# Reordering the last two pairs' products and changing how a list scheduler ranks what feeds small products, in a Winograd-like adaLN/FFN kernel

## The chip, the cores and the metric

The kernel runs on one NeuronCore of a Trainium2 chip. The metric is device time in microseconds of one execution; before the change the median of three runs is 460.26 us (460.14 to 460.26).

## The reference

All arrays are float32. `x` is 64 x 64 x 1024; each of the 64 batches has a condition number that picks one of sixteen 64 x 64 matrices.

```python
h = jnp.einsum('bct,bcd->bdt', x, cond_weights[condition])        # 64x64 matrix per batch
gate_logits = jnp.einsum('bsd,ed->bse', h, gate_w)                # 8 experts
weights, selected = jax.lax.top_k(gate_logits, 2)
w_full = sum(one_hot(selected) * softmax(weights))
low = jnp.einsum('bsd,erd->ebsr', h, lora_A)                      # 8 experts x rank 16
result = jnp.einsum('bsd,od->bso', h, base_w) + base_b
result += 2.0 * jnp.einsum('ebsr,eor,bse->bso', low, lora_B, w_full)
out = x + result
```

## The kernel before

**Tiling.** The 4096 tokens are 32 tiles of 128. The big product multiplies x (before the condition matrix, which is applied afterwards) with the 1160 columns of `lora_A`, `gate_w` and `base_w`, laid out as three column chunks of 384, 388 and 388. The contraction over 1024 is cut in four blocks of 256. float32 precision is kept by splitting each operand into a high and a low fp32r part: ScalarE (ACT) copies the high part (`xh`, `wh`, `zh`, line 234), VectorE (DVE) subtracts for the low part (`xl`, `wl`, `zl`, line 231), and TensorE (PE) does three matmuls for one product (line 414: high x high, low weight, low x).

**Plain tiles and pairs.** Tiles 0 to 3 are multiplied plainly, in the order of the list `PLAIN`: for tiles 0 and 1 the third column chunk takes the blocks in the order `LASTK = (3, 2, 0, 1)`, so its last weight block to arrive is `b23`. Tiles 4 to 31 go in 14 pairs (numbers 2 to 15) by a fast scheme with 20 products `p1` to `p20` for each pair. Each product is six matmuls of 388 (or 384) columns, in two halves. Four PSUM banks hold running sums, named X, Y, R and Q (`BANK`): several products of a pair add into one bank one after another. Between two of them an eviction takes the running sum out: DVE `mix` (line 740, writes `st`), ACT `keep` (line 719, writes `st`, recorded at line 234) or ACT `pass_on` (line 723, from bank to bank). The next product into the bank must wait for that eviction. In bank Y stand p19, p14, p15, p2, p8 and p9; an eviction follows each but p8. In bank X stand p16, p5, p17, p18, p3, p10 and p12.

**Small products.** When a chunk of z (the result of the big product) is complete, `chunk` splits it (`zh`, `zl`) and `post` applies the condition matrix (`bdh`, `bdl`) to it and adds the LoRA part: line 447, three to six matmuls into the banks `ps_a` and `ps_o`. Chunk 0 also feeds the gate (lines 486 to 493) and a transpose on PE (`tr`, line 500). `finish` (line 457) adds the result to the token tile `xtok`. The condition matrices are fetched by an indirect DMA from GpSimd (POOL, line 394, `bdr`) and split by `load_cond`: ACT `bdh`, DVE `bdl`. `load_tok` loads the x rows (SP, line 380) and adds the bias by DMA (POOL, line 381).

**What sets the order.** Nothing is ordered by the hardware: each engine executes its list of instructions in order, and waits at each for its operands. The lists are made when the program is built, by `Program.run`, a list scheduler with costs and due times written in the source. Each step gets a latest start `late` from the due times backwards through what depends on it. At every turn the engine that can start earliest takes, of its ready steps, one marked `first`, or else the one with the smallest `late`. The mark `first` is on the small products and transposes of tiles 0 to 29 (line 450 and `tr`); such a step is offered to PE only `MARGIN = 1.2` us after its operands are ready by the scheduler's own clock, and then goes ahead of the big products. Steps with `early` (loads and gathers) are offered not before `late - AHEAD`. The big products themselves are chained by the key `"order"`, so their order is exactly the hand-written list: `HEAD` and `TAIL` for pairs 2 to 13, and `FINAL` for the last two pairs, where `t` names a tail product of pair 14 and `p` a product of pair 15.

Of the kernel before, what the change touches and what calls it, by code (L numbers as in the profile page):

```python
# [41 lines left out]
PE, ACT, DVE, POOL, SP = "PE", "ACT", "DVE", "POOL", "SP"  # L42
# [4 lines left out]
ISSUE = 0.45  # L47
FLIGHT, DMA = 2.0, 1 / 360e3
QUEUE = 3.0
FIRST = 11.0  # L50
TWICE = 2.5
AHEAD = 10.0
MARGIN = 1.2
# [9 lines left out]
            p12="f9", p13="f13", p14="r", p15="f15", p16="a11", p17="a22", p18="f18", p19="f19", p20="f11")  # L63
BANK = dict(p6="R", p16="X", p7="Q", p5="X", p19="Y", p17="X", p11="R", p13="R", p18="X", p4="Q", p20="Q", p3="X",
            p1="R", p10="X", p12="X", p14="Y", p15="Y", p2="Y", p8="Y", p9="Y")
# [4 lines left out]

PARTS = ((2, slice(0, 200)), (2, slice(200, W)))

FINAL = "t14 p6 t15 p16 p7 t2 p5 t8 p17 t9 p11 p4 p13 p19 p18 p20 p14 p3 p10 p15 p12 p1 p2 p8 p9".split()

SPLITS = (("f6", "a11"), ("s", "f5"), ("f19", "a22"), ("f11", "f13"), ("f18", "a24"), ("f3", "f1"), ("a13", "f9"),
          ("r", "f15"), ("f2", "f8"))
# [3 lines left out]
class Program:  # L80
# [7 lines left out]
    def add(self, engine, cost, fn, reads=(), writes=(), due=None, first=False, size=0.0, early=None, port=False,  # L88
            after=0.0):

        n = len(self.steps)
        engine, cost = (e if isinstance(e, (list, tuple)) else [e] for e in (engine, cost))
        deps = set()
        for b in list(reads) + list(writes):
            if b in self.writer:
                deps.add(self.writer[b])
        for b in writes:
            deps.update(self.readers.get(b, ()))  # L100
        for b in reads:
            self.readers.setdefault(b, []).append(n)
        for b in writes:
            self.writer[b], self.readers[b] = n, []
        deps.discard(n)
        self.steps.append(dict(eng=dict(zip(engine, cost)), fn=fn, deps=deps, first=first, size=size, port=port,
                               lag=FLIGHT + QUEUE + size * DMA if size else 0.0, after=after,
                               due=self.horizon if due is None else due,
                               early=SP in engine and not reads if early is None else early))

    def run(self):
        steps, n = self.steps, len(self.steps)
        succ = [[] for _ in steps]
        for i, s in enumerate(steps):
            for d in s["deps"]:
                succ[d].append(i)
        hop = lambda a, b: SAME[a] if a == b else HOP[a]
        late = [0.0] * n
        for i in reversed(range(n)):
            s = steps[i]  # L120
            c, e = min(s["eng"].values()), next(iter(s["eng"]))
            late[i] = min([s["due"] - c] + [late[j] - hop(e, next(iter(steps[j]["eng"]))) - s["lag"] - c
                                            for j in succ[i]])
        left = [len(s["deps"]) for s in steps]
        ready, end, by = [0.0] * n, [0.0] * n, [None] * n
        free = dict(START)
        cand = {e: set() for e in HOP}

        def offer(i):
            for e in steps[i]["eng"]:  # L130
                t = max([steps[i]["after"]] + [end[d] + hop(by[d], e) for d in steps[i]["deps"]])
                if steps[i]["early"]:
                    t = max(t, late[i] - AHEAD)
                t += MARGIN if steps[i]["first"] else 0.0
                cand[e].add((i, t))

        for i in range(n):
            if not left[i]:
                offer(i)
        done, port, wire = 0, 0.0, 0.0  # L140
        while done < n:
            best = None
            for e, c in cand.items():
                if c:
                    t = max(free[e], min(max(r, port) if steps[i]["port"] else r for i, r in c))
                    if best is None or t < best[0]:
                        best = (t, e)
            t, e = best
            i, r = min(((i, r) for i, r in cand[e] if (max(r, port) if steps[i]["port"] else r) <= t + 1e-9),
                       key=lambda q: (not steps[q[0]]["first"], late[q[0]], q[0]))  # L150
            for f in steps[i]["eng"]:
                cand[f] = {q for q in cand[f] if q[0] != i}
            end[i], by[i] = t + steps[i]["eng"][e], e
            free[e] = end[i]
            if steps[i]["size"]:
                end[i] = wire = max(end[i] + FLIGHT, wire) + steps[i]["size"] * DMA
            if steps[i]["port"]:
                port = end[i]
            steps[i]["fn"](e)
            done += 1  # L160
            for j in succ[i]:
                left[j] -= 1
                if not left[j]:
                    offer(j)
        return max(end)
# [3 lines left out]
def cond_ffn_kernel(ctx, tc, xT, x, idx, cw, wall, bias, lb, out):  # L169
# [22 lines left out]
    eng = {ACT: nc.scalar, DVE: nc.vector, POOL: nc.gpsimd}  # L192
# [3 lines left out]
    def many(n, shape, dt, name):  # L196
        return [sb.tile(shape, dt, name=f"{name}{j}") for j in range(n)]
# [8 lines left out]
    bdr, bdh, bdl = many(2, [P, P], F32, "bdr"), many(2, [P, P], F32R, "bdh"), many(2, [P, P], F32R, "bdl")  # L206
# [21 lines left out]
    add = pr.add  # L228

    def sub(e, o, a, b):  # L230
        eng[e].tensor_tensor(o, a, b.bitcast(F32), ALU.subtract)  # L231

    def copy(e, o, a):
        (nc.scalar.copy if e == ACT else nc.vector.tensor_copy)(o, a)  # L234
# [7 lines left out]
    def tt_cost(n):  # L242
        return 0.08 + 0.00104 * n
# [94 lines left out]
    def mix_w(o, a, b, f, over):  # L338
# [3 lines left out]
        add(DVE, tt_cost(2 * W), lambda e: nc.vector.tensor_tensor(r.ap(), x.ap(), y.ap(), f),  # L342
            [k for z in (x, y) if z is not r for k in z.keys], r.keys, port=True, after=FIRST)

# [46 lines left out]
    def load_cond(i):  # L391

        j = i % 2
        add(POOL, 1.04, lambda e: nc.gpsimd.indirect_dma_start(  # L394
            out=bdr[j], out_offset=None, in_=cw,
            in_offset=bass.IndirectOffsetOnAxis(ap=rows[:, i:i + 1], axis=0)),
            ["rows"], [("bdr", j)], size=4.0 * P * P, early=True)
        add(ACT, 0.28, lambda e: copy(e, bdh[j], bdr[j]), [("bdr", j)], [("bdh", j)])
        add(DVE, 0.25, lambda e: sub(e, bdl[j], bdr[j], bdh[j]), [("bdr", j), ("bdh", j)], [("bdl", j)], port=True)


    due = {}
# [147 lines left out]
    for q in range(NPLAIN, NPAIR):  # L550
        if q == NPAIR - 2:
            ORDER += [(q + (p[0] == "p"), "p" + p[1:]) for p in FINAL]
            break
# [41 lines left out]
    add(POOL, 1.1, make_rows, writes=["rows"])  # L595
    add(POOL, 0.6, lambda e: make_identity(nc, ident), writes=["ident"])
    load_cond(0)
    load_cond(1)
    for k in LASTK:
        load_split_w(f"b{k + 1}3")  # L600
# [11 lines left out]
    def plain(i, c, k):  # L612
        if (i, k) not in xa0:
            us = xrs.two()
            for d in range(2):
                load_x(i, k + d, us[d])
            xa0[i, k], xa0[i, k + 1] = split_x(us)
            xrs.give(*us)
        if (i, c) not in zb:
            zb[i, c] = f"z{take('z', 4)}"  # L620
            if c == 0 and i > 1:
                load_cond(i)
        ks, m = LASTK if c == 2 and i < 2 else range(KQ), f"b{k + 1}{c + 1}"
        for f in range(2):
            zstep(("plain", i, c, k, f), zb[i, c], xa0[i, k], SINGLE.get(m, m), f, k == ks[0] and f == 0,
                  k == ks[-1] and f == 1, CN[c])
        left[i, k] -= 1
        if not left[i, k]:
            xas.give(xa0[i, k])
        if k == ks[-1]:  # L630
            post(i, c, split_z(CN[c], lambda: bank[zb[i, c]][:, :CN[c]], zb[i, c]))
            if c == 2:
                late_sum(i)
                store(i, range(3))
# [229 lines left out]
```

## Time and profile before

| | |
|---|---|
| median of three runs | 460.26 us |
| the profiled execution, as a run | 460.46 us |
| its span, first to last instruction | 458.7 us |
| outside of the span | 1.8 us |
| PE busy (matmuls) | 452.7 us, 99% |
| DVE busy | 383.5 us, 84% |
| ACT busy | 227.2 us, 50% |
| POOL busy | 89.6 us, 20% |
| granted TensorE clock | 1.000 |
| DMA traffic | 75.00 MB, mean 164 GB/s |

Times in the trace are microseconds from the start of the span. PE is the matmul row and PEld the row of weight loads, which runs ahead of it. A matmul is recorded with 0.34 us, but the next one starts 0.18 us later, since they overlap; so one reads the pace of PE from the starts. In brackets stands the idle time of an engine ahead of an instruction, with what ended it. Bank X is `ps_z` like all four; products are told apart by their weights: p10 is `wh_t_p` with 384 columns, p8 `wh_t_p` near the end, p9 `wh_g_p`, p15 `wh_h_p`.

### The profile page before, as it was taken

The numbers are of one execution on the slowest core, as the hardware profiler recorded it, in microseconds if no ns is written. First come the engines' busy times: TensorE is split into PE (matmuls) and PEld (weight loads), VectorE is DVE, ScalarE is ACT, GpSimd is POOL, SyncE is SP. The second block draws the span as 40 slices with busy tenths as digits, with TensorE's granted clock in tenths as the row PEclk, the third lists the DMA queues.
The fourth block names the chain that finished last, engine by engine and source line by source line (L and its number), as shares of the span: only waits on it lengthen the run. The fifth ranks groups of instructions, "written<-read, shape, count | busy, mean of one in ns | idle before, by whom it ended". The sixth has DMA issues, their size and how long they took to land.

```text
span 458.7 us, 7577 instructions
## 1 busy us (share of the span) xinstructions
PE 452.7 (99%) x2621; PEld 449.7 (98%) x2621; DVE 383.5 (84%) x941; ACT 227.2 (50%) x520; POOL 89.6 (20%) x107
## 2 busy tenths in 40 slices
PE   8999999999999999999999999999999999999995
PEld 8999999999999999999999999999999999999995
DVE  5999997879989788796987979789797988888674
ACT  5864666543736345373543646354454544546331
POOL 3030214121303021220303003030210403103000
PEclk9999999999999999999999999999999999999999
DMA  8932748977768462764847456565565746556142
GB/s 279 352 117 47 153 107 198 213 211 202 180 206 202 172 161 87 217 131 163 199 127 202 108 182 148 172 162 133 191 123 185 173 129 193 116 174 149 51 134 91
DMA packets 36229, 75.00 MB, mean 164 GB/s; under 512 B 4432, under 2 KB 22240, under 8 KB 36192
## 3 DMA queue, kind: packets, MB, share of 16 engines
q0 software_dynamic: 10560, 36.72, 33.5%
q1 hardware_dynamic: 25200, 37.32, 25.9%
q10 hardware_dynamic: 432, 0.49, 0.4%
q8 instruction: 20, 0.33, 0.3%
q14 instruction: 17, 0.14, 0.1%
HBM read 57.74 MB, written 16.78 MB: 162 GB/s over the span
## 4 chain that ended last, share of the span: by engine, by line
PE 97%; DMA 1%; DVE 1%; ACT 0%; issue 0%
PE ps_z L414 76%; PE ps_o L447 15%; PE ps_a L447 6%; DMA w_b<-in_w 1%; PE ps_a L500 1%; DVE wl_b_b L231 0%; DVE xtok L457 0%; DVE st L740 0%; ACT wh_b_b L234 0%; DVE xl L231 0%; PE ps_z L447 0%; DVE xh L234 0%
## 5 line engine op out<-in xcount | busy, mean ns | idle before, releaser
L231 DVE TENSOR_TENSOR xl<-xr,xh 128x512 fp32r<-128x512 f32 (+1 forms) x138 | 92.1, 670 | 20.0 <-ACT xh L234 19.8
L414 PE MATMUL ps_z<-wh_t_p,xh 128*128 128x388 f32 (+1 forms) x308 | 105.3, 342 | 0.1
L414 PE MATMUL ps_z<-wh_t_p,xl 128*128 128x388 f32 (+1 forms) x308 | 104.3, 339 | 0.0
L414 PE MATMUL ps_z<-wl_t_p,xh 128*128 128x388 f32 (+1 forms) x308 | 104.3, 339 | 0.0
L234 ACT CAST xh<-xr 128x512 fp32r<-128x512 f32 (+1 forms) x136 | 82.5, 610 | 37.2 <-PE ps_z L414 32.5
L740 DVE TENSOR_TENSOR st<-ps_z,st 128x388 f32<-128x388 f32 x126 | 70.2, 558 | 21.2 <-PE ps_z L414 20.2
L292 DVE TENSOR_TENSOR xr<-xr 128x256 f32<-128x256 f32 (+1 forms) x139 | 69.6, 526 | 3.6 <-DMA xr<-in_xT 3.4
L414 PE MATMUL ps_z<-wh_b_p,xh 128*128 128x388 f32 (+1 forms) x180 | 61.4, 341 | 0.0
L414 PE MATMUL ps_z<-wh_b_p,xl 128*128 128x388 f32 (+1 forms) x180 | 60.9, 338 | 0.0
L414 PE MATMUL ps_z<-wl_b_p,xh 128*128 128x388 f32 (+1 forms) x180 | 60.8, 338 | 0.0
L414 PEld LDWEIGHTS ps_z<-wh_t_p,xh 128*128 128x128 f32 x308 | 57.8, 188 | 1.2 <-DVE st L740 0.7
L414 PEld LDWEIGHTS ps_z<-wl_t_p,xh 128*128 128x128 f32 x308 | 57.9, 188 | 0.0
L414 PEld LDWEIGHTS ps_z<-wh_t_p,xl 128*128 128x128 f32 x308 | 57.9, 188 | 0.0
L464 POOL DMA_DIRECT2D out<-xtok x30 | 16.8, 560 | 193.6 <-DVE xtok L457 89.6
L234 ACT CAST zh<-st 128x388 fp32r<-128x388 f32 (+1 forms) x70 | 36.1, 517 | 22.1 <-DVE st L740 15.2
L381 POOL DMA_DIRECT2D xtok<-in_bias x28 | 27.0, 964 | 96.9 <-DMA xtok<-in_x 89.6
L394 POOL DMA_INDIRECT bdr<-in_cw,rows x32 | 36.9, 1155 | 26.4 <-DVE zl L231 17.7
L457 DVE TENSOR_TENSOR xtok<-ps_o,xtok 128x388 f32<-128x388 f32 (+1 forms) x56 | 30.9, 554 | 11.2 <-PE ps_o L447 10.7
L723 ACT ACTIVATE ps_z<-ps_z 128x388 f32<-128x388 f32 x42 | 20.1, 478 | 40.5 <-PE ps_z L414 39.4
L231 DVE TENSOR_TENSOR zl<-st,zh 128x388 fp32r<-128x388 f32 (+1 forms) x70 | 38.7, 554 | 0.9 <-ACT zh L234 0.6
L414 PEld LDWEIGHTS ps_z<-wh_b_p,xh 128*128 128x128 f32 x180 | 33.8, 188 | 0.2
L414 PEld LDWEIGHTS ps_z<-wl_b_p,xh 128*128 128x128 f32 x180 | 33.8, 188 | 0.0
(143 smaller groups left out, 873.0 us busy)
## 6 DMA issues: line engine op xcount, KB each, us to landing
xr<-in_xT SPq DMA_DIRECT2D x128, 128.0 KB, 3.2
xtok<-in_bias POOLq DMA_DIRECT2D x32, 512.0 KB, 7.1
out<-xtok POOLq DMA_DIRECT2D x30, 512.0 KB, 3.2
xtok<-in_x SPq DMA_DIRECT2D x28, 512.0 KB, 3.6
w_b<-in_w SPq DMA_DIRECT2D x10, 388.0 KB, 5.9
xtok<-in_x POOLq DMA_DIRECT2D x4, 512.0 KB, 6.6
out<-xtok SPq DMA_DIRECT2D x3, 194.0 KB, 2.2
bdr<-in_cw,rows POOLq DMA_INDIRECT x32, 5.3
```

The lines of the kernel that those rows point to most:

```text
L231: eng[e].tensor_tensor(o, a, b.bitcast(F32), ALU.subtract)
L234: (nc.scalar.copy if e == ACT else nc.vector.tensor_copy)(o, a)
L292: add(DVE, tt_cost(2 * P * len(os)), lambda e: nc.vector.tensor_tensor(some(xr, os), some(xr, xs), some(xr, ys), f), [("xr", u) for u in s ...
L381: add(POOL, 1.1, lambda e: nc.gpsimd.dma_start(xtok[j], bias.broadcast_to([P, T]), accum_op=ALU.add), writes=keys, size=TWICE * 4.0 * T * P)
L394: add(POOL, 1.04, lambda e: nc.gpsimd.indirect_dma_start(out=bdr[j], out_offset=None, in_=cw, in_offset=bass.IndirectOffsetOnAxis(ap=rows[ ...
L414: nc.tensor.matmul(z, l[:, j, n], w.ap()[:, f, :cols], start=(start and q == 0), stop=(stop and q == 2), skip_group_check=True)
L447: nc.tensor.matmul(d, l, r, start=(start and m == 0), stop=(stop and m == len(mms) - 1), skip_group_check=True)
L457: add(DVE, 0.09 + 0.00104 * (s.stop - s.start), lambda e: nc.vector.tensor_tensor(xtok[j][:, o], bank[b][:, s], xtok[j][:, o], ALU.add), [ ...
L464: add(POOL, 1.0, lambda e: nc.gpsimd.dma_start(out[i * P:(i + 1) * P, o], xtok[j][:, o]), src, size=4.0 * P * (o.stop - o.start))
L500: add(PE, 0.107, lambda e: nc.tensor.matmul(tp, low[i % 2][:, :ER], ident, is_transpose=True, start=False, stop=False, skip_group_check=True),
L723: add(ACT, 0.2 + 0.00085 * W, lambda e: nc.scalar.mul(z[b], z[x], scale), [BANKS[x]], [BANKS[b]])
L740: add(DVE, 0.09 + 0.00104 * W, lambda e: nc.vector.tensor_tensor(unit(u), a(), b(), f), reads, [ukey(u)])
```

## The change

Three edits. `FINAL` gets another order: p7 moves from before t2 to after t9, p17 from before t9 to after p7; p19 comes ahead of p4 instead of behind p13, p14 ahead of p11 instead of behind p20; p11 and p13 come later, p20 ahead of p18, and p15 stands ahead of p3 instead of between p10 and p12. The backward pass that makes `late` subtracts `MARGIN` at each step that is marked `first`, so all that feeds a small product of tiles 0 to 29 is ranked 1.2 us earlier for each such step on the way. And the two `bdh` copies of `load_cond` are offered to ACT at 16.0 us of the scheduler's clock at the earliest; only those of tiles 0 and 1 can be ready before that.

```diff
+CONDS = 16.0
...
-FINAL = "t14 p6 t15 p16 p7 t2 p5 t8 p17 t9 p11 p4 p13 p19 p18 p20 p14 p3 p10 p15 p12 p1 p2 p8 p9".split()
+FINAL = "t14 p6 t15 p16 t2 p5 t8 t9 p7 p17 p19 p4 p14 p11 p13 p20 p18 p15 p3 p10 p12 p1 p2 p8 p9".split()
...
-            late[i] = min([s["due"] - c] + [late[j] - hop(e, next(iter(steps[j]["eng"]))) - s["lag"] - c
+            late[i] = min([s["due"] - c] + [late[j] - MARGIN * steps[j]["first"] - hop(e, next(iter(steps[j]["eng"]))) - s["lag"] - c
                                             for j in succ[i]])
...
-        add(ACT, 0.28, lambda e: copy(e, bdh[j], bdr[j]), [("bdr", j)], [("bdh", j)])
+        add(ACT, 0.28, lambda e: copy(e, bdh[j], bdr[j]), [("bdr", j)], [("bdh", j)], after=CONDS)
```

In the built programs the order of every engine's list differs after this, not only for the last two pairs. The instructions are the same but for one DVE addition of 128x512 (`sum_x`, line 292), which becomes two of 128x256.

## The prediction

> **What bounds the kernel now.** I read the page's busy times and clock row first, then who the weight loads of PE wait for, then the chain of waits over the last 20 us, then the timelines at each place found.
>
> ```profile
> PE 452.7 (99%) x2621; PEld 449.7 (98%) x2621; DVE 383.5 (84%) x941; ACT 227.2 (50%) x520; POOL 89.6 (20%) x107
> PEclk9999999999999999999999999999999999999999
> L414 PE MATMUL ps_z<-wh_t_p,xh 128*128 128x388 f32 (+1 forms) x308 | 105.3, 342 | 0.1
> ```
>
> PE is busy 99% of the span at full clock, and the big products have 0.1 us of idle time ahead of them. The change removes no matmul, so the question is only how much PE idles. The waits of the weight loads, from the view of waits:
>
> ```profile
> PEld L225 <- DVE warm L311: 1.1, 1, 1.1
> PEld ps_z L414 <- DVE wl_b_b L231: 0.8, 2, 0.4
> PEld ps_z L414 <- DVE st L740: 0.7, 2, 0.4
> PEld ps_z L414 <- DVE xl L231: 0.2, 1, 0.2
> ```
>
> (us in total, times, longest). The first two lie before 7 us, while the first weights arrive, and the last at 11.5 us. Nothing else in 450 us is named but two waits for DVE's `st`, 0.7 us together. The chain of waits shows where they are, in the last pair:
>
> ```profile
> 437.91 1.60 PE ps_z L414 x9
> 439.51 0.02 issue
> 439.53 0.57 DVE st L740
> 440.10 0.04 issue
> 440.14 5.57 PE ps_z L414 x30
> 445.71 0.53 PE ps_a L447 x3
> 446.23 0.11 PE ps_a L500
> 446.34 0.02 issue
> 446.36 2.41 PE ps_z L414 x12
> ...
> 453.80 0.68 DVE xtok L457 x2
> ```
>
> Nine matmuls in 1.60 us: one each 0.178 us, so a product of six costs 1.06 us. At 439.53 p3 has ended in bank X, DVE takes the sum out for 0.57 us, and p10 into the same bank starts at 440.14. One group of small products (0.53 us) lies between; it hides part of 0.02 + 0.57 + 0.04 = 0.63 us plus the end of p3's last matmul. At 446.36 p8 starts behind p2's eviction in bank Y. The chain runs to the end on PE, then 0.68 us DVE and the last store.
>
> **The change, part by part.**
>
> *The new order of the last two pairs.* In the built order the two places that wait are as before: p10 is still directly behind p3 with the same group of three small matmuls between, and p8 still behind p2 with that group and the transpose. So 0.40 + 0.33 us of idle time stays, unless DVE comes to p3's eviction at another time. By the rows before: an eviction takes DVE 0.48 us from start to start (439.53 to 440.01), a `zl` 0.47, an `xl` of 512 columns 0.60, and DVE starts 0.2 us after the last matmul's slot of 0.178 us is over (439.16 + 0.178 to 439.53). Count from the end of p20's slot. The new DVE list is: evict p20 0.20 to 0.68, zl to 1.15, xl to 1.75, zl to 2.22, evict p15 (its product ends at 1.05 for p18 + 1.06 = 2.11, so from 2.31) to 2.79, xl for p10 to 3.39, and then p3's eviction, which could start at 3.17 + 0.20 = 3.37. It is late by 0.02 us. If one of these takes 0.1 us more, so does PE. The cost is +0.02 us, at best 0, at worst +0.15.
>
> What is spread out is p19, p14 and p15 of bank Y and p7 to p17. Which covers remain? p19 to p14 now has p4 between, 1.05 us, and needs 0.20 + 0.57 + 0.04 = 0.81: 0.24 to spare. p5 now follows p16 after t2 alone, 1.06 us, and needs ACT's `keep` of p16's sum (0.48 us, like the row of line 723) with a `zh` (0.47) that starts in front of it: about 0.96. p18 to p3 has p15 between, with ACT's pass done 1.75 us after p20, against 2.11. Before the change these places waited 0 as well, so nothing is won, and each costs 0 as long as its 0.1 to 0.36 us to spare lasts. Cost 0; between 0 (none can gain, as none waited) and +0.3.
>
> *The margin in the rank.* It moves instructions in all lists. On PE, of 166 small groups 72 stand at the same place between the half products and 44 one half product away, a few up to nine. No small product waited before, so pulling their inputs forward wins nothing on PE. What it can cost is what DVE and ACT do later. The view of waits has for ACT:
>
> ```profile
> ACT bdh L234 <- PE ps_o L447: 30.7, 14, 4.0
> ACT bdh L234 <- DMA bdr<-in_cw,rows: 1.0, 1, 1.0
> ```
>
> ACT stood 31 us at the head of its list behind a `bdh` copy, up to 4.0 us at one time. The Trainium skill (TensorE: Matmul & The Clock Gate, Part 1, section on the architectural detail of the array) says that ACT's and DVE's queues are strictly first in, first out, so such a wait holds up all behind it; a rank that pulls these copies forward would then be paid for with up to 4.0 us at a place. The rows say that PE lost nothing by these 15 waits, as ACT is 50% busy and works ahead. I take the rows: 0, and keep the rule for a rival.
>
> One place does change for the worse, at the head. Before:
>
> ```profile
> 24.77 0.84 ACT L234 CAST wh_b_b<-w_b 128x776 fp32r<-128x776 f32 x1 [1.30 <-DMA w_b<-in_w]
> 25.91 0.95 DVE L231 TENSOR_TENSOR wl_b_b<-w_b,wh_b_b 128x776 fp32r<-128x776 f32 x1
> 26.26 0.33 PE L447 MATMUL ps_a<-zh,bdh 128*128 128x384 f32 x1
> 26.78 0.34 PE L414 MATMUL ps_z<-wh_b_b,xh 128*128 128x388 f32 x1
> 26.96 0.40 PE L414 MATMUL ps_z<-wl_b_b,xh 128*128 128x388 f32 x1
> ```
>
> `b23`, the last weight block, is split on ACT when its DMA lands (24.77), then on DVE, and its first product starts at 26.78 behind three small matmuls; the second matmul, which reads `wl`, is held 0.06 us. In the new PE list these three small matmuls come behind the first half of that product. PE is then at it at 26.26 and wants `wl` at 26.44. The new DVE list has `wl` ahead of a `zl`: it starts at 25.61 + 0.04 = 25.65, not at 25.91, and is there at 25.65 + 0.95 + 0.04 = 26.64. That is a wait of 0.20 us, and after a wait the first matmul takes 0.10 us longer (440.14 to 440.42: 0.28 instead of 0.18). So 0.30 against 0.06: +0.24 us. If the DMA lands 0.2 us sooner it is 0, if later by that, +0.45.
>
> SP issues the 512 KB of `lb` now behind four x loads of 128 KB: at the 390 GB/s of this stretch 1.3 us later than its landing before 20.73, so 22.0. ACT reads it in the new list after two `zh`, near 22.6, for 1.06 us, and comes to `b23` by 23.7, before 24.77. Cost 0 unless it lands after 23.8. POOL's first instructions, the gathers of tiles 0 and 1 among them (6.87 and 8.23 us), keep their order.
>
> *The two copies held to 16 us.* They come after the last `xh` of the head, at 16.2 us. With the longest landing of a gather, 7.3 us, the second is there at 15.5. Two casts of 0.29 us, of which one was in front before: ACT has 1.3 us of idle at 23.5. Cost 0; up to +0.1. The addition in two parts costs DVE about 0.1 us more, with 2.5 us idle near 431: 0.
>
> The sum against the profiled execution: 460.46 + 0.02 + 0.24 = 460.72, and its span 458.7 to 459.0. That execution lies 0.20 above the median of 460.26, so the median becomes 460.5.
>
> **A second rule.** The same page of the Trainium skill, in its section on a second failure of the clock gate, tells that short idle times of PE while banks are cycled can make the clock fall back to half. By that the waits in the last pair would cost far more than their length: the 14 us from 440 to 454 at half clock would be 14 us, and a new order with shorter or longer gaps there would move the time by much. The row of the stretch that has both waits says otherwise:
>
> ```profile
> 439.00:447.00 8.00, 7.86 (x43) 7.24 (x42) 5.98 (x20) 3.31 (x10) 0.88 (x1) 1.00 0.48 116
> ```
>
> Granted clock 1.00. So a wait costs its length and 0.1 us, and I price all so.
>
> **The rivals.** *Spreading pays (0.10).* If p3's and p2's evictions are met earlier, because DVE is freer there than I count, both waits go: 460.5 - 0.7 = 459.8. For it: it is all that PE idles late. Against it: both pairs of products still stand next to each other. Even then it is 0.1% and not 0.2%; only with the head's waits gone too (another 0.8) would it be, and nothing in the change touches those.
>
> *A thin cover breaks in every pair (0.10), slower.* In pairs 2 to 14 p1 lies between p3 and p10. The trace has p3's eviction end 0.15 to 0.31 us ahead of p10 in 12 of those 13 pairs (411.70 and 411.92 in the last), of which 0.04 is the handing over. If the new rank puts one more `zl` of 0.47 us ahead of that eviction, it is short by 0.47 - 0.18 = 0.29, with the restart 0.39, in 12 pairs 4.7 us: 460.3 + 4.7 = 465. It decides from 0.18 us. Against it: in the built order the instruction ahead of the eviction is the 512-column `xl` in 10 of the 13 pairs, where it was before in 11, and in the other three bank Q's eviction, which is due earlier; and DVE is idle 16% of the time.
>
> *The late `lb` (0.05), slower.* If its landing slips from 22.0 to 25 us, ACT, first in first out, has `lbh` ahead of `b23`, whose copy starts at 26.1 instead of 24.77: +1.3 and the 0.24, 461.8. It decides from 23.8 us.
>
> **How the numbers follow.** Forecast 0.75: 460.5, by itself 460.0 to 460.9 from the bounds above. Two in ten may be left out: the range goes down to the first rival and up to near the late `lb`, 459.8 to 461.5. A measurement of this kernel can tell about 0.2%, 0.92 us: faster is below 459.34, slower above 461.18. Faster 0.04, from more than the first rival; slower 0.15, from the other two; within 0.81.
>
> **What would show it.** Right: two waits for `st` of 0.3 to 0.5 us in the last 20 us; a wait for `wl_b_b` of about 0.2 to 0.3 us near 26.4; no other wait of PE for DVE or ACT after 27 us. Wrong: a row of waits of PE for `st`, many times (the broken cover); `lbh` after 24 us; or the two late waits gone. The forecast falls if the order of the lists matters by way of something that this trace does not show, such as DMAs that land later because SP or POOL issue them in another order.

## The result, and the profile after

| | before | after |
|---|---|---|
| median of 22 runs each, same chip | 460.28 us | 461.06 us |
| ratio | | 1.0013, 95% interval 1.0007 to 1.0019 |
| the profiled execution, as a run | 460.46 us | 460.79 us |
| its span | 458.7 us | 458.3 us |
| median span, all runs | 458.4 us | 458.65 us |
| median time less span | 1.8 us | 2.42 us |

(The median span and time less span of before are those of the repeat described under the experiments.) The change makes the kernel slower by 0.13% by the ratio, and by 0.78 us (0.17%) by the two medians: clear of the noise, but within the 0.2% that I had called no change. It has two parts: 0.25 us more between the first and the last instruction, and 0.6 us more outside of them. (Their sum is 0.87 and not 0.78 us, as the spans of before are from another job.) The second part is not in my sum at all.

The page of the changed kernel (its lines stand one number higher than before) has the same busy times, and PE waits for DVE's `st` in two places, as before. First a line of the page, then two of the view of waits:

```profile
PE 452.6 (99%) x2621; PEld 450.1 (98%) x2621; DVE 384.0 (84%) x942; ACT 227.7 (50%) x520; POOL 89.7 (20%) x107
```

```profile
PEld L226 <- DVE warm L312: 1.1, 1, 1.1
PEld ps_z L415 <- DVE st L741: 0.8, 2, 0.5
```

There is no wait for `wl_b_b` in this one execution; executions of other kernels with the same head have one (below). The chain of waits of the last pair is the DVE list that I had counted, piece for piece:

```profile
437.11 0.56 DVE st L741
437.67 0.47 DVE zl L232
438.14 0.60 DVE xl L232
438.74 0.47 DVE zl L232
439.21 0.02 issue
439.23 0.56 DVE st L741
439.79 0.60 DVE xl L232
440.39 0.48 DVE st L741
440.87 0.04 issue
440.91 4.50 PE ps_z L415 x24
```

p20's eviction, `zl`, `xl`, `zl`, p15's eviction, `xl`, p3's eviction, then p10 on PE at 440.91. DVE has no gap of more than 0.02 us in it, so it is DVE and no longer only p3's end that sets p10's start; the two coincide. The DMA view of the stretch from 458.3 to 462 us, after the last instruction of the program, holds one transfer:

```profile
DMA packets 1, 0.01 MB, mean 2 GB/s; under 512 B 0, under 2 KB 0, under 8 KB 0
...
q14 instruction: 1, 0.01, 1.0%
```

This is a fetch of instructions, 8192 bytes, which starts at 460.5 and ends at 461.0 us. In the kernel before the same view, from 458.7 to 462 us, is empty; its last fetch of that size on this queue is at 424.6 us:

```profile
DMA packets 0, 0.00 MB, mean 0 GB/s; under 512 B 0, under 2 KB 0, under 8 KB 0
```

### The profile page after: what moved, and what is told of

The parts are those of the page before. It is cut to its first block, busy times and chain, and to the rows that moved or that the text cites. A ratio compares the mean times of both kernels' runs of the same rounds, so it can differ in the third digit from the quotient of the medians.

```text
span 458.3 us, 7596 instructions
## 1 busy us (share of the span) xinstructions
PE 452.6 (99%) x2621; PEld 450.1 (98%) x2621; DVE 384.0 (84%) x942; ACT 227.7 (50%) x520; POOL 89.7 (20%) x107
## 4 chain that ended last, share of the span: by engine, by line
PE 98%; DVE 1%; issue 0%
PE ps_z L415 75%; PE ps_o L448 15%; PE ps_a L448 6%; PE ps_o L226 1%; PE ps_a L501 1%; DVE st L741 0%; DVE xl L232 0%; DVE zl L232 0%; DVE xtok L458 0%; PE ps_z L448 0%; DVE ltl L219 0%; DVE low L222 0%; DVE warm L312 0%
```

## The experiments

Each ran beside the kernel before, on one chip. "Outside" is the median of time less span. To compare stretches I also add up the excess of PE's slots. It is for every matmul the time to the start of the next one, less the usual pitch (0.014 us and 0.000418 us for each column; 0.1 us for a transpose), where that is over 0.04 us.

**The kernel before, again.** For the spread.

> The kernel before, unchanged, as a control. The profile of after has a span of 458.3 us, no longer than the 458.7 of before, while the median is 461.06 against 460.28: outside of the span lie 2.1 to 2.5 us in 22 runs of after, and 1.8 in the one profiled execution of before. Theory A (the loss is outside of the span, ahead of the first or behind the last instruction): spans here about 458.7 in all runs, 1.6 to 1.9 us outside. Theory B (the one profile of before was long in its span by chance, at the head, where the first loads arrive; the loss is inside): spans here of 457.8 to 458.2 on the median, 2.2 to 2.5 us outside. Ratio 1.000 either way.

460.20 us, ratio 1.0 (0.9992 to 1.0008); spans 458.0 to 459.3, median 458.4; outside 1.80 in every run within 0.06. In this profile the waits at 11.5 and 26.96 us of my first profile are absent: the head varies by some tenths from run to run, the outside does not. So 0.6 us outside is a difference of the programs.

**Only the new order.**

> Only the new order of the last two pairs' products. By the prediction: p10 waits as before or 0.02 us longer, p8 as before, so 460.3, ratio 1.000. Theory B with the tail as its place: ratio 1.001, with p10 later by 0.3 to 0.6 us and the span longer by as much. If the loss comes from the rank: 1.000.

```diff
-FINAL = "t14 p6 t15 p16 p7 t2 p5 t8 p17 t9 p11 p4 p13 p19 p18 p20 p14 p3 p10 p15 p12 p1 p2 p8 p9".split()
+FINAL = "t14 p6 t15 p16 t2 p5 t8 t9 p7 p17 p19 p4 p14 p11 p13 p20 p18 p15 p3 p10 p12 p1 p2 p8 p9".split()
```

464.82 us, ratio 1.0098 (1.0073 to 1.0123), outside 1.77. The six runs lie between 461.96 and 466.08 us, so the size is rough. One DVE addition, two matmuls and one stretch of the profiled run tell why (timelines of DVE and of PE, then the busy times by stretch with the granted clock behind POOL's column):

```profile
418.86 0.43 DVE L292 TENSOR_TENSOR xr<-xr 128x256 f32<-128x256 f32 x1 [2.82 <-DMA xr<-in_xT]
```

```profile
418.74 0.34 PE L414 MATMUL ps_z<-wh_t_p,xl 128*128 128x388 f32 x1
421.21 0.45 PE L414 MATMUL ps_z<-wh_b_p,xh 128*128 128x388 f32 x1 [2.13 <-DVE st L740]
```

```profile
422.30:425.80 3.50, 3.50 (x13) 3.50 (x12) 2.39 (x9) 2.02 (x6) 0.00 (x0) 0.51 0.80 150
```

DVE, in order, waits 2.82 us for an x block; the chain of waits leads from its landing at 418.84 back to 412.98, where an `xl` that read the slot before ends. Behind it in the list are the `zl`, the `xl` and the eviction that the next product into the bank needs. PE stands from 418.92 to 421.21, and then the granted clock is half for 3.4 us (0.51 over the stretch; its matmuls start 0.32 us apart instead of 0.18), which costs another 1.7 us. In the changed kernel, with the new ranks, DVE does its additions of that stretch (413.0 to 416.6 us) without a wait.

**Only the margin in the rank.**

> Only the margin in the rank, without holding the two condition copies to 16 us. ACT then has both copies in front of weight splits at the head, while the gathers (issued at 6.9 and 8.2 us) have not landed, so PE waits near 11 us: by the landing times of 2.5 to 7.3 us the copies come at 10 to 15.5, and PE waits 1 to 4 us: 461.5 to 464.5. If ACT's work ahead covers it: 460.3.

```diff
-            late[i] = min([s["due"] - c] + [late[j] - hop(e, next(iter(steps[j]["eng"]))) - s["lag"] - c
+            late[i] = min([s["due"] - c] + [late[j] - MARGIN * steps[j]["first"] - hop(e, next(iter(steps[j]["eng"]))) - s["lag"] - c
```

464.92 us, ratio 1.0103 (1.0089 to 1.0118), outside 1.91. The timelines of ACT and PE at the head, and the stretch behind:

```profile
8.28 0.40 ACT L234 CAST xh<-xr 128x256 fp32r<-128x256 f32 x1
12.94 0.30 ACT L234 CAST bdh<-bdr 128x128 fp32r<-128x128 f32 x1 [4.26 <-DMA bdr<-in_cw,rows]
```

```profile
14.34 0.64 PE L414 MATMUL ps_z<-wh_b_b,xh 128*128 128x384 f32 x1 [2.77 <-ACT xh L234]
```

```profile
14.40:17.90 3.50, 3.43 (x10) 2.92 (x11) 3.50 (x6) 3.50 (x8) 0.38 (x1) 0.51 1.04 393
```

The rank pulls the first `bdh` copy ahead of an `xh` (in the kernel before it stands at 15.12 us and waits for nothing). ACT stands 4.26 us at it until the gather lands, PE idles 2.8 us for the `xh` behind it, and again runs 3.4 us at half clock: 3.1 (the wait of its weight load) + 1.7 = 4.8 us, against 4.7 measured.

**Margin and the hold to 16 us, old order.**

> The margin in the rank and the hold to 16 us, with the old order of the last two pairs. If the loss of 0.6 us comes from the rank (small products elsewhere, other lists on all engines): 460.9, ratio 1.0013. If it comes from the new order: 460.3, ratio 1.000. By the prediction: PE waits 0.24 us at 26.4, ratio 1.0005.

461.05 us, ratio 1.0018 (1.0010 to 1.0027), span 459.1, outside 1.98. The hold takes away 3.9 us of the 4.7. What is left in the span is a wait at the head, on PE's timeline,

```profile
26.04 0.34 PE L414 MATMUL ps_z<-wh_b_b,xh 128*128 128x388 f32 x1
26.63 0.44 PE L414 MATMUL ps_z<-wl_b_b,xh 128*128 128x388 f32 x1 [0.25 <-DVE wl_b_b L231]
```

(0.59 us from start to start instead of 0.18: `b23`'s wait, as forecast) and 0.22 us at 416.8, which is not there with the new order. The order alone costs 4.6 us, the rank alone 4.7, rank and hold 0.85, all three 0.8. So the rank needs the hold, and the order needs at least one of the other two, by the trace the rank (order and hold without the rank were not run).

**POOL's list made longer.** The fetch behind the end could belong to any engine whose list has changed. POOL's list has grown from 181 to 192 instructions, all of it separate waits for semaphores.

> The changed kernel with 16 memsets of 128x1 put at the end of POOL's list, behind its last DMA issue; no other list changes. Theory: 0.6 us of the change's 0.8 lie outside the span, because POOL's list has grown from 181 to 192 instructions and its next block of 8192 bytes (128 instructions) is now fetched only after the last instruction, at 460.5 us; the 16 memsets bring that fetch forward into the last products, where nothing waits for it. Then time less span falls from 2.4 back to about 1.8 us, the median from 461.06 to about 460.45, and the last fetch of 8192 bytes lies before 457 us. Rival: the fetch belongs to another engine, or the time outside has another cause: 461.06 and 2.4 us as before.

> The kernel before with 11 memsets of 128x1 at the end of POOL's list, which makes it as long as in the changed kernel (192 instructions). Theory of the fetch: a fetch of 8192 bytes appears after the end of the span, time less span rises from 1.78 to between 2.0 and 2.5 us, and the median from 460.2 to 460.4 to 460.9. Rival (another engine or cause): 460.2, time less span 1.78.

```diff
     pr.run()
+    pad = sb.tile([P, 1], F32, name="pad")
+    for _ in range(16):
+        nc.gpsimd.memset(pad, 0.0)
```

(16 in the changed kernel, 11 in the kernel before.) In the changed kernel: 460.67 us, ratio 1.0013 (1.0005 to 1.0022) to a before of 460.14; span 458.7 as without, outside 1.97 instead of 2.42. The fetch has moved from 460.5 to 440.4 us, which is while POOL executes the memsets (its timeline):

```profile
439.57 2.77 POOL L827 MEMSET pad<- 128x1 f32 x16
```

So it is POOL's block, and 0.45 of the 0.62 us outside go with its late fetch; the other 0.17 us stay, and why is open. In the kernel before with 11 memsets: no fetch behind the end, 460.27 us, outside 1.90. There the length alone (192) did not bring it; 0.1 us came anyway.

**lb loaded after b23.**

> The changed kernel with the 512 KB load of lb issued after the load of b23 instead of ahead of it. Theory: the 0.25 us that the span has grown is the wait for wl_b_b of b23 near 26.4 us; with b23 landing some 1.3 us sooner (512 KB at 390 GB/s) the wait is gone: median span about 458.35 instead of 458.65, no row of a wait for wl_b_b near 26 us, median time about 460.75 with the time outside unchanged. Rival: the span's 0.25 us is spread over other places or is drift from run to run: span 458.6 and 461.06.

```diff
-    add(SP, ISSUE, lambda e: nc.sync.dma_start(xtok[2], lb), writes=lraw, size=4.0 * T * P)
+    add(SP, ISSUE, lambda e: nc.sync.dma_start(xtok[2], lb), writes=lraw, size=4.0 * T * P, after=17.5)
```

460.04 us, ratio 0.9999 (0.9991 to 1.0007). The span fell from 458.65 to 458.3. In this pair of profiles `b23`'s copy on ACT starts at 23.88 us against 24.20, 0.3 us sooner and not 1.3, and 0.22 us of wait for `wl_b_b` are still there. One profile can't decide, but there are four of each head:

| head | start of `b23`'s copy | excess at its product |
|---|---|---|
| `lb` ahead (changed; with 16 memsets; margin and hold; p1 moved) | 24.20, 24.58, 24.73, 25.07 us | 0, 0.33, 0.52, 0.93 us |
| `lb` later (this one and the three below that build on it) | 23.88, 23.37, 23.36, 23.48 us | 0.22, 0, 0, 0 us |

With `lb` ahead the copy starts later the later `b23` lands, and the wait grows with it. With `lb` later it starts 1.1 us sooner on average, near the 1.3 forecast. So `lb`'s place decides how often the wait comes, and the wait is large enough for the span's 0.25 us; more than that four profiles can't show. Not foreseen was that the time outside fell from 2.42 to 1.77: as a side effect the scheduler gave POOL 191 instructions, and no fetch follows the end. Whether that is the reason, or `lb`'s place, the next run tells:

> The kernel with lb loaded after b23 (460.04 us, span 458.3, time less span 1.77, POOL's list 191 instructions, no fetch behind the end) with two memsets of 128x1 at the end of POOL's list: 193 instructions. Theory of the fetch: two instructions that take POOL some 0.1 us, long before the end, bring the fetch of 8192 bytes back behind the span's end; time less span 1.9 to 2.5 us, median 460.2 to 460.75. Rival (it was the place of lb's load that took the time outside away): 460.04, time less span 1.77.

The same kernel with two memsets at the end of POOL's list: 460.56 us (1.0006, 0.9998 to 1.0015), outside 2.04, and the fetch is back at 460.7 us. Two instructions cost 0.27 us outside. The other 0.2 us is in the span (458.5 against 458.3), where the profile has 0.5 us of waits near 10 to 12 us, which vary from run to run.

> The kernel before with 13 memsets of 128x1 at the end of POOL's list (194 instructions); with 11 (192) no fetch appeared behind the end, and the time was 460.27 with 1.90 us outside of the span. Theory of the fetch: two instructions more bring it: a fetch of 8192 bytes after the end of the span, time less span 2.0 to 2.5 us, span unchanged at 458.4, median 460.4 to 460.9. Rival (the fetch behind the end needs the other lists of the changed kernel too): 1.90 us and 460.27 as with 11.

The kernel before with 13 memsets instead of 11: a fetch at 460.4 us, span 458.5 and outside 1.99 (13 runs, 1.85 to 2.06) against 1.79 of before in the same job (17 runs, 1.74 to 1.84). In the sum it disappears in the spread: 460.42 to 460.36, ratio 1.0003 (0.9995 to 1.0012). All together:

| kernel | POOL's instructions | last fetch of 8192 bytes, after the span's end | outside |
|---|---|---|---|
| before | 181 | none | 1.80 us |
| order only | 181 | none | 1.77 |
| lb later | 191 | none | 1.77 |
| lb later, p8 covered (below) | 191 | none | 1.80 |
| lb later, p10 covered (below) | 191 | none | 1.90 |
| before + 11 | 192 | none | 1.90 |
| margin only | 192 | none | 1.91 |
| changed | 192 | starts 2.2 us after | 2.42 |
| changed, p1 moved | 192 | 2.5 us after | 2.46 |
| margin and hold | 193 | 1.8 us after | 1.98 |
| lb later + 2 | 193 | 1.8 us after | 2.04 |
| before + 13 | 194 | 1.8 us after | 1.99 |
| changed + 16 | 208 | none (440.4 us) | 1.97 |

Up to 191 instructions no fetch is late. At 193 and 194 it is, and 0.2 us more lie outside; at 192 it is either absent or later still, and then 0.6 us more. What makes the difference at 192, and the 0.1 to 0.2 us that four kernels have without a late fetch, stays open.

**Covers for the two late waits.** Both waits for `st` are left in the changed kernel. First p1 between p3 and p10:

> The changed kernel with p1 moved between p3 and p10 in the order of the last two pairs. Theory: p10's wait of 0.40 us for DVE's st is a cover that is missing, and p1 (1.06 us) covers it: one wait for st is left (p8 behind p2), span 458.65 to about 458.25, median 461.06 to about 460.65. Rival: the wait comes back at another place, since p12 now ends 1.06 us later and the gate's chain of chunk 0 behind it has only p2, p8 and p9 as cover, and DVE is as late for p2's eviction: 461.06 or up to 0.5 us more.

```diff
-FINAL = "t14 p6 t15 p16 t2 p5 t8 t9 p7 p17 p19 p4 p14 p11 p13 p20 p18 p15 p3 p10 p12 p1 p2 p8 p9".split()
+FINAL = "t14 p6 t15 p16 t2 p5 t8 t9 p7 p17 p19 p4 p14 p11 p13 p20 p18 p15 p3 p1 p10 p12 p2 p8 p9".split()
```

462.66 us, ratio 1.0051 (1.0037 to 1.0064), span 460.2. p10 no longer waits, but p12 ends one product later, and the gate's chain behind it (the steps on DVE and ACT from chunk 0 to the transpose and on to `lth`) has only three products as cover, so PE stands at both of its ends (timeline):

```profile
449.63 0.30 PE L500 MATMUL ps_a<-ident,low 128*128 128x128 f32 x1 [0.68 <-DVE mx L486]
450.29 0.44 PE L447 MATMUL ps_o<-lbh,lth 128*128 128x388 f32 x1 [0.36 <-ACT lth L234]
```

PE's excess of the last 45 us is 2.15 us instead of 0.95. The rest of the longer span is the head's wait for `wl_b_b`, 0.93 us in this profile.

Then two others on the kernel with `lb` later (460.04 us), which keep four products behind p12:

> The kernel with lb loaded after b23, and the end of the order of the last two pairs written as p18 p20 p3 p15 p10 p12 p1 p2 p8 p9: p20 covers p18 to p3, p15 covers p3 to p10, and four products still follow p12 as in the changed kernel; the small products of condition matrix times chunk 0 of the last two tiles are marked first, or the scheduler would put the gate's chain behind everything. Theory: p10's wait of 0.40 us is gone and nothing takes its place: one wait for st (p8), span 457.9, median about 459.65. Rival: the end is set by the gate's chain (low, mx, e, wf, low, transpose) of the last tile, and any move of evictions on DVE there comes back as a wait of PE for low or lth: 460.0 to 460.5.

> The kernel with lb loaded after b23, with p1 moved between p2 and p8 at the end (p12 p2 p1 p8 p9), and the small products of chunk 0 of the last two tiles marked first as in the run beside it. p10 stays directly behind p3. Theory: p8's wait of 0.33 us is gone, p10's of 0.40 stays; span 458.0, median about 459.75. Rival: the small group of tile 30, which now stands one product later, makes the transpose wait for the gate's chain: 460.0 to 460.6.

```diff
-FINAL = "t14 p6 t15 p16 t2 p5 t8 t9 p7 p17 p19 p4 p14 p11 p13 p20 p18 p15 p3 p10 p12 p1 p2 p8 p9".split()
+FINAL = "t14 p6 t15 p16 t2 p5 t8 t9 p7 p17 p19 p4 p14 p11 p13 p18 p20 p3 p15 p10 p12 p1 p2 p8 p9".split()
...
-            first=i < NT - 2)
+            first=i < NT - 2 or (c == 0 and not with_lora))
```

The second run has the same mark, and `p10 p12 p2 p1 p8 p9` at the end of the order of the changed kernel. 460.73 us (1.0011, 1.0002 to 1.0019) and 460.90 us (1.0017, 1.0011 to 1.0024), 0.7 and 0.9 us slower than their base. The views of waits of the two:

```profile
PEld ps_z L414 <- DVE st L740: 0.6, 1, 0.6
PEld ps_o L447 <- ACT lth L234: 0.5, 1, 0.5
```

```profile
PEld ps_o L447 <- ACT lth L234: 0.7, 1, 0.7
PEld ps_z L414 <- DVE st L740: 0.5, 1, 0.5
PEld ps_o L447 <- DVE xtok L457: 0.4, 1, 0.4
```

In each the wait that was to go is gone. The other for `st` stays, and a new one for `lth`, the end of the gate's chain, is there. PE's excess of the last 45 us is 0.94 us in their base, 1.20 with p10 covered, 1.79 with p8 covered. With p8 covered that is the loss; with p10 covered it is 0.26 of 0.7 us, 0.13 lie outside, and the rest is not placed. (The mark was not run by itself.) No version beat the kernel before by what can be measured.

## Why the prediction was right, and where its sum was not

**The verdict.** Within 0.2%, 461.06 us in the range of 459.8 to 461.5. But it is above the 460.0 to 460.9 that the forecast gave by itself. It lies in the range only because I had widened it for the late `lb`, which did not come: in that much the range was luck. The likeliest value of 460.5 was 0.56 us too low, all of it from a term that I had carried over and not costed.

**The order, +0.02 us: right.** PE's excess of the last 45 us is 0.96 us in both profiles of before and 0.95 and 0.94 with all three edits. My DVE count from p20's eviction to the end of p3's was 3.67 us (3.39 + 0.48 less 0.20); the chain has 440.87 - 437.11 = 3.76. p10 is still held, for 0.29 us and 0.11 for the restart, p8 for 0.18 and 0.11 (0.40 and 0.29 us, where I had 0.40 and 0.33).

**The spread, 0: right for the change, not by itself.** Between 39 and 413 us the excess is 2.38 us before and 2.40 after. But the order alone costs 4.6 us, since, by its profile, an x load comes late for it under the old ranks. I had looked at which products cover which evictions, and not at which `xl` frees the slot of which later load.

**The margin in the rank and the hold, each 0: right only as a pair.** I priced the rank at 0 because ACT's 31 us of waits at `bdh` cost PE nothing, and the hold at 0 as well. The rows that I took were all after 27 us, where ACT works ahead. At the head it does not. There the first in, first out rule of the Trainium skill (TensorE: Matmul & The Clock Gate, Part 1), which I kept for a rival, decides: without the hold ACT stands 4.26 us and the kernel loses 4.7 us. The hold is what the price of 0 rests on.

**The head, +0.24 us: right in the mechanism, with too narrow bounds.** The median span grew by 0.25 us. The four profiles with this head show 0 to 0.93 us for the wait and its restart, where I had 0 to 0.45. It follows the landing of `b23`, as I had it. But I had PE come to the product at 26.26 us, from the one trace of before; in these four it comes at 25.97 to 26.08, so that the same landing costs 0.2 to 0.3 us more than I counted. That the median still came out is in part luck. ACT reads `lb` at 22.34 us in the changed kernel, 0.3 us before I had it, and in all four profiles it waits 0.8 to 1.05 us for `b23` after that. So `lb` did not hold up ACT; what it takes is the DMA's time ahead of `b23`.

**The outside, carried over at 1.8 us: the step that failed.** It is 2.42. In the profiled execution the sum looks right (460.72 forecast, 460.79 measured) only because two errors cancel: the span was 458.3 and not 459.0, the outside 2.5 and not 1.8. That is luck. Nothing in the trace of before announces the fetch; but the built lists, which I had, show that POOL's grew by 11. My last sign, an effect of the lists that this trace does not show, named POOL's order of issue; it was the length of its list. The Trainium skill (Runtime: NRT & Kernel Launch, Instruction fetch mechanics) says that a sequencer fetches the next block while it executes the present one, so that the cost is mostly hidden. For the fetches within the span the runs agree: PE's excess between 39 and 413 us is the same with and without the moved blocks. One that falls behind the last instruction had nothing left to hide it, and 0.2 to 0.6 us came with it. The traces show blocks of 8192 bytes on this queue (q14) and of 16384 on the other instruction queue (q8); the page has 16 KiB for all engines.

**The rivals.** Spreading did not pay: both waits stayed. A thin cover did not break in any pair. `lb` was not late. The second rule (the clock) was rightly set aside for waits of 0.3 to 0.5 us: granted clock 1.00 from 437 to 447 us. What idle times of 2 to 3 us do to the clock shows in two of the experiments.

## What to carry to other kernels

When a scheduler makes the lists, edits that look independent may not be. Run each alone, or a pair that cancels is taken for two harmless parts. A trace in which an engine's waits cost nothing says so only for the stretch they are in; at the head, where ACT has no lead, one early copy behind a gather cost 1%. And read the time outside of the span for every version: it moved by 0.6 us with, for the most part, one block of instructions of an engine that was busy for 20% of the span.

## What was not expected of the hardware

- The granted clock halves sooner than the Trainium skill's table has it (TensorE: Matmul & The Clock Gate, Why this matters for your kernels: gaps of more than about 3 us are to be avoided). One idle time of 2.1 to 2.3 us (421.21 us, order alone) was enough, and one of 2.8 us (14.34 us, rank alone). Each time the clock was at half for 3.4 us (0.51 over a stretch of 3.50), and 1.7 us were lost on top of the wait. Waits of up to 1.0 us (p1 moved) left it at 1.00. Between 1.0 and 2.1 us nothing was measured.
- The end of the execution moves with the end of a fetch of instructions. In the five profiles with a late fetch it ends 2.76, 2.80, 2.33, 2.39 and 2.29 us behind the span (changed; p1 moved; margin and hold; lb later + 2; before + 13), and the time less the span of these executions is 2.52, 2.55, 2.09, 2.15 and 2.05 us: 0.24 or 0.25 less in each. It does not follow the fetch's start (2.19, 2.49, 1.84, 1.82 and 1.78 us) as closely. That the execution waits for this fetch is the plain reading, and not more: why the time ends 0.24 us ahead of the fetch's record is open.
